# Fixed roles for the banks of PSUM in an attention kernel, with scores in pairs and singles

## The chip, the core and the metric

The kernel runs on one core of a Trainium2 chip. The core has a matrix engine (TensorE, "PE" in the profile, with its weight loads as "PEld"), a vector engine (VectorE, "DVE"), a scalar engine (ScalarE, "ACT"), a general engine (GpSimd, "POOL") and a queue that issues most DMAs (SyncE, "SP"). Matrix products land in PSUM, which has eight banks; one bank holds 512 fp32 values in each of 128 partitions. DVE and ACT read PSUM and write SBUF. The metric is the device time of one execution in microseconds (us); lower is better.

## The reference

The input `x` is 8 sequences of 1024 tokens with 256 features, in fp32. One layer of attention and one feed-forward layer with three-valued weights, each between two layer norms:

```python
x = x + _layernorm(attn(_layernorm(x)))
x = x + _layernorm(ffn(_layernorm(x)))

# attn: 16 heads of 16 features, 4 key/value heads, each shared by 4 query heads
q, k, v = x @ Wq, x @ Wk, x @ Wv          # then rotary embedding of q and k
scores = einsum('bhqd,bhkd->bhqk', q, k) / sqrt(256)
p = softmax(scores, axis=-1)
o = einsum('bhqk,bhkd->bhqd', p, v)        # then o @ Wo

# ffn: weights are +1, 0 or -1 by a threshold
out = einsum('bsd,od->bso', x, ternary(weight) * alpha) + bias
```

## The kernel before

**Units, blocks, steps.** The 8 sequences are cut into 16 units of 512 tokens. A unit has 4 blocks of 4 query heads; a block has 8 steps, one for each 128 keys; a step has 4 score tiles of 128 keys by 512 queries, one for each key/value head. So there are 64 blocks and 2048 score tiles, numbered by `s`.

**Scores are computed twice.** The softmax subtracts each row's maximum. For this a first pass (`max_scores`, line L582, tiles `sm`) makes 128 queries by 512 keys at a time and DVE takes the maximum of each row (`TENSOR_REDUCE`, L607). When a block has all its maxima, they are joined (`mc`, L624), transposed on PE (`shift_rows`, tile `pm`, L630), split in a high and a low part (`mh`, `ml`) and written by a DMA as extra rows into the stacked queries `q_st`. The second pass (`exp_scores`, L655, tiles `se`) then makes 128 keys by 512 queries with the shift already taken off, and ACT takes the exponential (`exp_one`, L671) into an SBUF tile `e`. `av_piece` (L691) multiplies `e` with the values into one PSUM bank `av`; `av_out` (L704) copies it out at the end of a block. There are 2048 matmuls for maxima and 2048 for exponentials. Each uses 64 rows of the array (the other 64 belong to the other pair of key/value heads, index `a`), so two that stand side by side with different `a` run at the same time.

**Groups.** `window(s)` writes out one group: two or three exponentials, as many matmuls for maxima between them, then perhaps one part of other work, then the `av` products of the group two before. PE, DVE and ACT execute exactly in the order in which the Python code calls them. `window_size` takes three exponentials, or two if a part that needs a PSUM bank is ready. Such parts ("banked") come from the projection of a later unit (`x`, `kv_and_dram`, `q`, `v`), from the tail of an earlier one (`attn`, `x`, `ffn`) and from `shift_rows`. The lists `P_PARTS` and `T_PARTS` give the step at which each part becomes ready. `maxima_by` keeps the maxima 40 to 52 score tiles ahead of the exponentials. From `s = 40` on (`REGULAR`) a group takes at most one banked part, and only if it has two exponentials; the last 13 steps have no maxima and take four exponentials at a time (`exp_two`). POOL and SP are ordered by a scheduler, with the hint `issue_after` for DMAs.

**PSUM.** Two tiles of two banks (`sm`) hold scores for maxima, each tile two matmuls; three single banks (`se`) hold scores for exponentials and, in turn with them, the results of banked parts; one bank is `av`. If a group ends between the two matmuls of an `sm` tile, `reduce_early` has DVE reduce the first half by itself, and the second half later.

The code follows with the profile's line numbers.

## Time and profile before

| | |
|---|---|
| median of 3 runs | 1646.88 us (1641.69 to 1648.25) |
| the profiled execution's own time | 1642.63 us |
| its span, first to last instruction | 1640.8 us |
| PE busy | 1579.7 us (96%) |
| DVE busy | 1399.3 us (85%) |
| ACT busy | 1274.8 us (78%) |
| POOL busy | 835.4 us (51%) |

A line of the profile's table of groups names the source line, the engine, the operation, the tile written and the tiles read, the shape, and how often it ran; after the bar stand the busy time of the group, the mean duration of one in ns, and the idle time of the engine just before, with what ended it. PE is pipelined: a matmul's recorded duration is longer than its turn, and the distance from one start to the next is what counts. In a timeline, the first column is the start in us and the second the time from the first start to the last end of the instructions merged into that line.

### The profile page before, as it was taken

What the parts mean: (1) busy time and instruction counts of PE and PEld (TensorE: products, weight loads), DVE (VectorE), ACT (ScalarE), POOL (GpSimd) and SP (SyncE); (2) the same over time, 40 slices, a digit from 0 to 9 for tenths busy, and PEclk for the clock granted to TensorE, in tenths of its full rate; (3) what the DMA queues carried; (4) which work ended last, traced back from release to release, by engine and by line L of the source; (5) the groups of instructions that cost most, each with busy time, mean ns of one, the idle gap of its engine ahead of it and who ended that gap; (6) DMA issues with size and microseconds to landing.
All of it is one profiled execution on the core that took longest, in us unless ns stands there. A gap on an engine that the chain in (4) does not pass through costs nothing.

```text
span 1640.8 us, 37250 instructions
## 1 busy us (share of the span) xinstructions
PE 1579.7 (96%) x14712; PEld 818.5 (50%) x14712; DVE 1399.3 (85%) x2049; ACT 1274.8 (78%) x2479; POOL 835.4 (51%) x1239
## 2 busy tenths in 40 slices
PE   7999999999999999999999999999999999999997
PEld 5544455454545545454544545455454544444544
DVE  7778788889898888989889898988989888898964
ACT  4657778878787887878788787887878787877884
POOL 5532457374653737455373835547374552323363
PEclk8989999999999999999999999999999999999999
DMA  4151425125151422515133251513325151231100
GB/s 139 53 101 34 91 77 101 59 76 101 56 106 49 91 67 82 101 46 105 60 83 75 77 106 44 104 49 89 71 67 104 40 97 42 46 70 34 42 15 27
DMA packets 86079, 117.99 MB, mean 72 GB/s; under 512 B 12088, under 2 KB 50808, under 8 KB 85752
## 3 DMA queue, kind: packets, MB, share of 16 engines
q1 hardware_dynamic: 85904, 115.60, 29.9%
q8 instruction: 116, 1.90, 0.5%
q14 instruction: 59, 0.48, 0.1%
HBM read 68.65 MB, written 45.88 MB: 70 GB/s over the span
## 4 chain that ended last, share of the span: by engine, by line
PE 80%; DVE 10%; DMA 3%; ACT 2%; POOL 2%; issue 2%; SPq 1%; POOLq 0%; DVEq 0%; ACTq 0%
PE av L691 28%; PE se L655 28%; PE sm L582 9%; DVE mx L607 7%; PE pa L283 3%; PE pq L283 2%; PE pf L283 2%; PE pt_ot L267 2%; ACT e L671 2%; PE pt_xt L267 2%; PE pkv L283 2%; DMA q_st<-ml 1%; DMA k_rot<-d_k 1%; PE pm L630 1%; DMA dk<-ks 1%
## 5 line engine op out<-in xcount | busy, mean ns | idle before, releaser
L607 DVE TENSOR_REDUCE mx<-sm 128x2 f32<-128x1024 f32 (+1 forms) x1304 | 1205.3, 973 | 191.9 <-PE sm L582 174.1
L671 ACT ACTIVATE e<-se 128x512 f32<-128x512 f32 x1996 | 1058.2, 602 | 223.0 <-PE sm L582 172.4
L582 PE MATMUL sm<-k_st,q_st 64*128 64x512 f32 x2048 | 748.4, 450 | 6.9 <-DVE mx L607 3.9
L655 PE MATMUL se<-q_st,k_st 64*128 64x512 f32 x2048 | 705.5, 441 | 26.7 <-ACT e L671 14.4
L691 PE MATMUL av<-e,v_aug 128*32 128x256 f32 (+3 forms) x8608 | 607.2, 378 | 0.0
L655 PEld LDWEIGHTS se<-q_st,k_st 64*128 64x128 f32 x2048 | 324.9, 185 | 405.7 <-ACT e L671 302.1
L582 PEld LDWEIGHTS sm<-k_st,q_st 64*128 64x128 f32 x2048 | 326.1, 185 | 65.1 <-DVE mx L607 41.9
L691 PEld LDWEIGHTS av<-e,v_aug 128*32 128x32 f32 x8608 | 194.4, 108 | 211.0 <-issue 148.3
L241 POOL TENSOR_SCALAR lnsc<-mv 128x2 f32<-128x2 f32 (+1 forms) x134 | 25.8, 193 | 400.1 <-DVE mv L239 395.1
L765 POOL TENSOR_TENSOR xn<-xn,a 128x512 f32<-128x512 f32 x30 | 38.4, 1282 | 131.8 <-DMA a<-d_rec 101.2
L826 POOL TENSOR_TENSOR a<-a,bias_bc 128x512 f32<-128x512 f32 x30 | 38.6, 1287 | 108.3 <-ACT a L825 108.3
L242 POOL TENSOR_TENSOR lnsc<-lnsc,mhalf 128x2 f32<-128x2 f32 (+1 forms) x134 | 92.5, 691 | 0.9
L162 POOL TENSOR_TENSOR hl<-xn,hl 128x512 fp32r<-128x512 f32 x60 | 76.5, 1287 | 0.4
L253 POOL TENSOR_SCALAR xn<-x,lnsc 128x256 f32<-128x256 f32 x116 | 65.1, 570 | 2.2
L237 DVE BATCH_NORM_STATS2 bnst<-a 128x6 f32<-128x256 f32 x120 | 44.5, 413 | 4.6 <-POOL a L826 4.6
L297 POOL TENSOR_TENSOR t<-q_rot,sin_q_sb 128x512 f32<-128x512 f32 x31 | 39.9, 1288 | 15.5 <-ACT q_rot L439 15.4
L283 PE MATMUL pa<-woh,hl 128*128 128x256 f32 x240 | 46.2, 294 | 1.1 <-ACT e L671 1.1
L283 PE MATMUL pq<-xt,wqkvh 128*128 128x256 f32 x256 | 45.8, 303 | 0.5 <-ACT e L671 0.5
L237 DVE BATCH_NORM_STATS2 bnst<-x 128x6 f32<-128x256 f32 x124 | 45.9, 412 | 0.4 <-DMA x<-in_L_attn_x 0.4
L271 ACT CAST ot<-pt_ot 128x512 fp32r<-128x512 f32 x66 | 39.6, 601 | 4.7 <-PE pt_ot L267 4.7
L439 ACT COPY q_rot<-pq 128x512 f32<-128x512 f32 x32 | 18.8, 586 | 30.9 <-PE pq L283 30.9
L162 POOL TENSOR_TENSOR hlq<-q_rot,hlq 128x512 fp32r<-128x512 f32 x31 | 39.8, 1285 | 4.8 <-ACT hlq L159 4.5
(157 smaller groups left out, 1303.1 us busy)
## 6 DMA issues: line engine op xcount, KB each, us to landing
q_st<-dq SPq DMA_DIRECT2D x90, 256.0 KB
dq<-hlq SPq DMA_DIRECT2D x60, 256.0 KB
d_av<-avsb SPq DMA_DIRECT2D x60, 256.0 KB
x<-in_L_attn_x SPq DMA_DIRECT2D x15, 512.0 KB
xn<-d_av SPq DMA_DIRECT2D x30, 256.0 KB
a<-d_rec SPq DMA_DIRECT2D x30, 256.0 KB
xr<-in_L_attn_x SPq DMA_DIRECT2D x15, 512.0 KB
out_x<-a SPq DMA_DIRECT2D x30, 256.0 KB
```

The costliest lines, as they stand in the source:

```text
L162: eng.tensor_tensor(lo, src, hi.bitcast(F32), ALU.subtract)
L237: nc.vector.bn_stats(st[:, t, :], src[:, t, :])
L242: nc.gpsimd.tensor_tensor(sc[:, 1, :], sc[:, 1, :], mhalf[:, :n], ALU.pow)
L253: eng.tensor_scalar(dst[:, t, :], src[:, t, :], sc[:, 0, t : t + 1] if eng is nc.gpsimd else mv[:, t, 0:1], sc[:, 1, t : t + 1], ALU.add i ...
L267: nc.tensor.transpose(pt[:, c, t * P : (t + 1) * P], src[:, t, c * P : (c + 1) * P], ident_r)
L283: nc.tensor.matmul(out, chunk(left[i], c), chunk(right[j], c), start=(k == 0), stop=(k == len(steps) - 1),)
L297: eng.tensor_tensor(dst, x, table.unsqueeze(1).to_broadcast(list(x.shape)), ALU.mult)
L582: scores = nc.tensor.matmul(sm[0][:, part, :], queries[rows], k_st[(u // UPB) % 3][rows, r2, ch * 512 : (ch + 1) * 512], start=True, stop= ...
L607: early[0] = nc.vector.tensor_reduce(mx[i][:, a, head_and_tile(i, r2, t), lo:n], sm[0][:, lo:n, :], AX.X, ALU.max).ins
L655: nc.tensor.matmul(sc if len(queries.shape) == 2 else sc.rearrange("p (j t) -> p j t", j=G), k_st[(i // G // UPB) % 3][rows, r2, kt * P : ...
L671: nc.scalar.activation(e, sc, AF.Exp, scale=1.0 / D**0.5)
L691: nc.tensor.matmul(av_ps[0][32 * r : 32 * r + 32, lo:hi], va[:, kt, r, :], es[i * NK + kt, r // 2, r % 2][:, lo:hi], start=(kt == 0 and lo ...
```

## The change

The eight banks get fixed roles: one two-bank tile for a pair of scores for maxima (`PAIR_M`, tag `s2`, one buffer), two single banks for single scores for maxima (`ONE`, tag `s1`), one two-bank tile for a pair of scores for exponentials (`PAIR_E`, tag `e2`, one buffer), one single bank for a third exponential or a part's result (`ALONE`, tag `se`), and `av`. The exponential of a pair is one ACT instruction of 128x1024. A group makes its pair of exponentials first, then the pair for maxima, then the single ones. `maxima_of` says how many maxima a group takes: beside one of the parts in `LONG` a group of two takes four (two pairs), other groups of two take two, and groups of three take what is then missing, one at least. The choice of the maxima's order (`pairs`, `singles`) is kept in lists. Some projection parts become ready a few steps later, and from unit 5 on two of them (`kt`, `q_to_dram`) issue their DMAs behind the latest shift.

```diff
-    ep = ctx.enter_context(tc.tile_pool(name="ep", bufs=12))
-    avp = ctx.enter_context(tc.tile_pool(name="avp", bufs=5))
+    ep = ctx.enter_context(tc.tile_pool(name="ep", bufs=4))
+    ep2 = ctx.enter_context(tc.tile_pool(name="ep2", bufs=6))
+    avp = ctx.enter_context(tc.tile_pool(name="avp", bufs=2))
...
-    ps_mx = ctx.enter_context(tc.tile_pool(name="ps_mx", bufs=2, space=PSUM))
-    ps_e = ctx.enter_context(tc.tile_pool(name="ps_e", bufs=3, space=PSUM))
+    ps_mx = ctx.enter_context(tc.tile_pool(name="ps_mx", bufs=1, space=PSUM))
+    ps_s = ctx.enter_context(tc.tile_pool(name="ps_s", bufs=2, space=PSUM))
+    ps_e = ctx.enter_context(tc.tile_pool(name="ps_e", bufs=1, space=PSUM))
...
-    spare = [1]
+    ALONE, ONE = (ps_e, "se"), (ps_s, "s1")
+    PAIR_E, PAIR_M = (ps_e, "e2"), (ps_mx, "s2")
+    spare = [[ALONE, ONE, PAIR_E, ONE, PAIR_M], 0]
...
+    def max_one(a, sm=None):
+        open_block()
...
+        if sm is None:
+            sm = ps_s.tile([P, 512], F32, tag="s1", name=f"s1_{a}_{i}_{t}_{r2}_{ch}")
+        max_scores(item, a, sm)
+        x = head_and_tile(i, r2, t)
+        nc.vector.tensor_reduce(mx[i][:, a, x, ch : ch + 1], sm, AX.X, ALU.max)
+        block_ends(i)
+        return a
+
+    def max_two(a, place=None):
+        open_block()
+        pool, tag = place or PAIR_M
+        sm = pool.tile([P, 2, 512], F32, tag=tag, name=f"s2_{taken[0]}")
...
+        for k in range(2):
+            max_scores(item, (a + k) % 2, sm[:, k])
+        x = head_and_tile(i, r2, t)
+        nc.vector.tensor_reduce(mx[i][:, :: -1 if a else 1, x, ch], sm, AX.X, ALU.max)
+        block_ends(i)
...
-    def exp_one(s):
...
-        nc.scalar.activation(e, sc, AF.Exp, scale=1.0 / D**0.5)
+    def exps_of(s, n, place=None):
+        pool, tag = place or (ALONE if n == 1 else PAIR_E)
+        shape = [P, 2, 512] if n == 2 else [P, 512]
+        sc = pool.tile(shape, F32, tag=tag, name=f"se_{s}")
+        e = (ep2 if n == 2 else ep).tile(shape, F32, tag=f"e{n}", name=f"e_{s}")
+        for k in range(n):
+            step, (r2, a) = (s + k) // 4, divmod((s + k) % 4, 2)
...
+            exp_scores(step, r2, a, sc[:, k] if n == 2 else sc)
         nc.scalar.activation(e, sc, AF.Exp, scale=1.0 / D**0.5)
...
-        (26, "begin", 0), (33, "x", 0, 0), (34, "x", 0, 1), (37, "begin", 1), (43, "x", 1, 0),
-        (45, "x", 1, 1), (49, "kv_and_dram"), (51, "q", 0), (52, "kt"), (53, "v"), (55, "q", 1),
-        (57, "q_to_dram"),
+        (30, "begin", 0), (35, "x", 0, 0), (36, "x", 0, 1), (37, "begin", 1), (43, "x", 1, 0),
+        (45, "x", 1, 1), (49, "kv_and_dram"), (51, "q", 0), (54, "kt"), (53, "v"), (55, "q", 1),
+        (62, "q_to_dram"),
...
-        (1, "fetch"), (7, "invert"), (8, "scale", 0), (9, "scale", 1), (12, "attn", 0),
+        (2, "fetch"), (7, "invert"), (8, "scale", 0), (9, "scale", 1), (12, "attn", 0),
...
+            behind = [behind_latest] if u > 4 and p[0] in ("kt", "q_to_dram") else []
+            at(start + k, *behind, part, projects, u, *p)
...
+    LONG = ("kv_and_dram", "q", "attn", "ffn")
+    AHEAD = 4
+
+    def maxima_of(s, size):
+        time = min(maxima_by(s + size), 4 * NSTEP)
+        n = time - taken[0]
+        if s < REGULAR:
+            return max(0, n)
+        if size == 2:
+            part_ = next((p for p in ready if banked(*p)), None)
+            far = part_ and not at_hand() and part_[0] is part and part_[1][2] in LONG
+            n = 4 if far and taken[0] + 4 <= time + AHEAD else 2
+        else:
+            n = max(1, n)
+        return min(n, 4 * NSTEP - taken[0])
...
         if late:
-            for r2 in range(2):
-                exp_two(s // 4, r2)
+            spare[0] = [ALONE, ONE, ONE]
+            for k in range(0, size, 2):
+                exps_of(s + k, min(2, size - k), PAIR_M if k else None)
         else:
-            end = min(maxima_by(s + size), 4 * NSTEP)
-            for q in range(max(size, end - maxima[0])):
-                if q < size:
-                    exp_one(s + q)
-                if maxima[0] < end:
-                    max_scores(maxima[0])
-                    maxima[0] += 1
-                if q == 0:
-                    take_low()
-            reduce_early(maxima[0])
+            n = maxima_of(s, size)
+            exps_of(s, 2)
+            take_low()
+            half = s % 2
+            if n >= 2:
+                max_two(half)
+                n -= 2
+            if size == 3:
+                exps_of(s + 2, 1)
+            else:
+                half = 1 - half
+            while n:
+                if n == 2:
+                    max_two(1 - half)
+                    break
+                half = max_one(1 - half)
+                n -= 1
...
+        spare[0] = [ALONE]
         while s < 8:
             s = window(s)
```

## The prediction

> **What bounds the kernel now.** I read the page first, for shares and the chain.

> ```profile
> PE 1579.7 (96%) x14712; PEld 818.5 (50%) x14712; DVE 1399.3 (85%) x2049; ACT 1274.8 (78%) x2479; POOL 835.4 (51%) x1239
> ...
> PE 80%; DVE 10%; DMA 3%; ACT 2%; POOL 2%; issue 2%; SPq 1%; POOLq 0%; DVEq 0%; ACTq 0%
> ```

> PE sets the pace and DVE is close behind; ACT has room. Second, the groups by form, for the price of one instruction:

> ```profile
> L671 ACT ACTIVATE e<-se 128x512 f32<-128x512 f32 x1996 | 1058.2, 602 | 223.0 <-PE sm L582 172.4 <-PE se L655 31.8
> L607 DVE TENSOR_REDUCE mx<-sm 128x2 f32<-128x1024 f32 x712 | 855.3, 1216 | 167.5 <-PE sm L582 153.2 <-PE se L655 11.0
> L607 DVE TENSOR_REDUCE mx<-sm 128x1 f32<-128x512 f32 x592 | 381.9, 680 | 24.5 <-PE sm L582 20.9
> ```

> A reduction of a pair takes 1.216 us, a half 0.680. Third, the waits, for what PE waits for:

> ```profile
> PEld se L655 <- ACT e L671: 302.1, 651, 0.9
> ...
> PEld sm L582 <- DVE mx L607: 41.9, 127, 1.4
> ...
> PE se L655 <- DMA q_st<-ml: 9.9, 8, 3.1
> ```

> The first is mostly no loss: the weight load waits while the av products still run. The second is real: over the whole run PE waits only 41.9 us for a maxima bank. Fourth, the timeline of PE, for the length of a group (first se to first se):

> ```profile
> 1003.28 0.50 PE L655 MATMUL se<-q_st,k_st 64*128 64x512 f32 x1
> 1003.29 0.50 PE L582 MATMUL sm<-k_st,q_st 64*128 64x512 f32 x1
> 1003.62 0.48 PE L655 MATMUL se<-q_st,k_st 64*128 64x512 f32 x1
> 1003.62 0.48 PE L582 MATMUL sm<-k_st,q_st 64*128 64x512 f32 x1
> 1004.10 0.74 PE L283 MATMUL pkv<-xt,wqkvh 128*128 128x256 f32 x4
> ...
> 1006.50 0.50 PE L655 MATMUL se<-q_st,k_st 64*128 64x512 f32 x1
> 1006.51 0.50 PE L582 MATMUL sm<-k_st,q_st 64*128 64x512 f32 x1
> 1006.84 0.39 PE L655 MATMUL se<-q_st,k_st 64*128 64x512 f32 x1
> 1006.84 0.62 PE L582 MATMUL sm<-k_st,q_st 64*128 64x512 f32 x2
> 1007.07 0.39 PE L655 MATMUL se<-q_st,k_st 64*128 64x512 f32 x1
> 1007.40 0.85 PE L691 MATMUL av<-e,v_aug 128*32 128x384 f32 x8
> 1008.18 0.49 PE L655 MATMUL se<-q_st,k_st 64*128 64x512 f32 x1
> ```

> Two scores run side by side (1006.50 and 1006.51); the next two follow after 0.34 us, the third two after 0.23, other work 0.33 after the last. av takes 0.78 here (1007.40 to 1008.18), 0.57 for 256 columns. So a plain group (three exponentials, three maxima) needs 1.68 us of PE, or 1.46 with the shorter av, and the long one at 1003.28 took 3.22. And DVE beside it:

> ```profile
> 1005.37 0.74 DVE L237 BATCH_NORM_STATS2 bnst<-a 128x6 f32<-128x256 f32 x2
> 1006.03 0.30 DVE L239 BATCH_NORM_AGGREGATE mv<-bnst 128x2 f32<-128x6 f32 x2
> 1007.30 1.23 DVE L607 TENSOR_REDUCE mx<-sm 128x2 f32<-128x1024 f32 x1 [0.97 <-PE sm L582]
> ```

> The reduction starts at 1007.30, 0.46 us after its second score's start (1006.84); DVE idled 0.97 beside the long part. Cutting all PE rows so, I count 449 plain groups, mean 1.806; of groups of two, 13 with pkv (mean 3.21), 26 pq (3.22), 31 pa (2.99), 28 pf (2.55), 61 pm (1.655), 109 with a transposition (1.98), 29 without a part (1.56), 13 ptv (1.47). A plain group's maxima cost DVE 1.73 start to start (1.131 a pair, 0.597 a half), about PE's 1.68: plain groups are where DVE binds, long ones where it idles.

> **The change part by part.** The changed order keeps the cuts between groups and their parts. Instead of 449 plain groups it has 367 with three maxima and 81 with one; 81 groups of two take four maxima (28 pa, 14 pf, 13 pkv, 12 pq, 14 pm); some 229 groups of two keep one pair. Matmuls and maxima are the same in number.

> (A) The 81 groups with four. Both pairs are written to the one s2 tile, so the second waits for DVE's reduction of the first, and all of PE's queue stands behind it: the long part, the av products, the next group. First pair at 0.34; reduction 0.46 later, at 0.80; it ends at 2.02; the second pair starts 0.05 later (a matmul started at 1010.03 after a reduction that ended at 1009.98), at 2.07; the part 0.33 later, at 2.40. Before, the part started at 0.66. That is 1.74 us per group, 81 x 1.74 = +141 us. Bounds: 1.41 if the second pair's own 0.33 is given back whole (+114), 2.34 if DVE is a single reduction late (0.60) on arrival (+190).

> (B) The 81 groups of three that then take one maximum use no s2; PE needs 0.34 + 0.33 + 0.57 or 0.78 = 1.24 to 1.45. The pair tile for exponentials has one buffer too: 0.53 from the matmul to ACT (1006.50 to 1007.04), about 1.01 for 128x1024 (an estimate: copies of 256 and 512 columns take 380 and 586 ns, so 0.41 more for 512 more), 0.05 to the next: 1.60. I take 1.51 against 1.806, -24 us; bounds 1.24 (-46) and 1.60 (-17).

> (C) The 367 plain groups. One s2 tile makes a round of 0.46 + 1.216 + 0.054 = 1.73 from pair to pair, and the single reduction just fits beside the pair's fetch; DVE's other work comes on top. That is 141 us in all (244 statistics x 0.33, 256 aggregates x 0.11, the 64 joins, 64 low parts and 15 reciprocals); half in these groups is 0.19 each, some of it beside waits. I take 1.86 against 1.806: +20. Bounds 1.73 (-28) and 1.90 (+34).

> (D) Groups of two with one pair meet the round of 1.73 as well: pm +0.08 x 47, no part +0.17 x 29, ptv +0.26 x 13, the rest is longer already; +12, bounds 0 and +25.

> (E) `av_out` puts its copy (0.47 start to start) ahead of the pair's exponential 63 times: 1.60 + 0.47 = 2.07 against a group of 1.8. Three buffers hid this; with one it costs up to 0.27 each. Half meets a wait for s2 anyway: +10, bounds 0 and +25.

> (F) Before `s = 40` all parts share one bank instead of three, several in one group: +8, bounds 0 and +15.

> (G) Moved steps. `begin 0` (two statistics and two aggregates on DVE, seven instructions on POOL), `kt` (six on POOL, ten DMAs on SP), `q_to_dram` (four DMAs) and the tail's `fetch` (three) come later. q_st is reloaded some 35 steps after `q_to_dram`, and k_st is read some 60 after `kt`, so SP's and POOL's delay is hidden; at one step of about 2.9 us that cover is over 100 us. Keeping these DMAs out of the shift's way can win at most the 9.9 us row: -5, bounds -10 and 0. The fewer SBUF tiles cost nothing: an avsb buffer is reused two blocks later (some 46 us, for one DMA of 256 KB), a pair of `e` six groups later, and its last av product comes four groups later. If av fell two groups further behind, that cover would be gone and ACT would wait a group.

> (H) Merging exponentials saves ACT 0.956 - 0.89 = 0.07 a pair, some 735 times, 48 us of ACT's time. ACT is 78% busy and 2% of the chain: nothing, and a pair's first half is now released 0.4 later, which stands in B and E.

> Sum: 141 - 24 + 20 + 12 + 10 + 8 - 5 = +162 us. The profiled execution took 1642.6 us (span 1640.8 and 1.8 around it), 4.3 under the median of the runs; 1642.6 + 162 = 1805, on the median 1809.

> [...] The rows say that two tiles of maxima left 41.9 us of waits in 2048 scores. [...] For ACT, the rows of H give 0.07 us a merge. [...]

> **The rivals.** (1) A milder loss: after each stall DVE and ACT have caught up, so B and C fall to their lower ends, and A to its own: 114 - 46 - 28 + 12 + 10 + 8 - 5 = +65, 1712. For it: DVE's 0.97 of idle beside the pkv group. Against: the round of 1.73 leaves no group with a pair below it. (2) Faster: the four maxima beside a long part do what DVE's idle time invites. If the second pair waited little, A would be 81 x 0.23 = 19, and with B at -46, C at -28, the rest nil and G at -5, -60: 1587. It decides at a wait where A is below 79 us, 0.97 us a group; the reduction alone is 1.22. (3) ACT's one pair tile binds: exponentials that follow a copy of a part (0.59) also miss the next group, some 160 times 0.3, +48: 1857. (4) The change doesn't do what it says: if the part is rarely beside the four, A vanishes; but the order shows all 81.

> Stalls might also cost clock. Here PEclk stays at 9 after the third slice, through a 3.06 us gap of PE at 198.5 us; the new ones are 1.4. [...]

> **How the numbers follow.** Forecast case 0.70; rival 1 0.14; rival 2 0.05; rival 3 0.08; rival 4 or no change 0.03. The range runs from rival 1 to beyond rival 3, 1705 to 1870, and leaves out rival 2, rival 4 and what exceeds A's upper bound. Faster by over 0.5% (about what a measurement here can tell) 0.06, within it 0.02, slower 0.92.

> **What will show it.** Right: PE waits for DVE before the second pair, some 1.3 us, in 81 groups, over 100 us in all against 41.9; PE's and DVE's busy shares fall together; plain groups stay near 1.8. Wrong: that wait below 50 us, plain groups at 1.68 or less, or a large new wait of se for ACT.

## The result and the profile after

| | before | after |
|---|---|---|
| median | 1646.95 us (4 runs, 1641.69 to 1648.25) | 1885.14 us (4 runs, 1882.93 to 1888.08) |
| ratio, 95% interval | | 1.1454 (1.1425 to 1.1484) |
| span of the profiled execution | 1640.8 us | 1881.1 us |
| granted TensorE clock, mean | 0.989 | 0.954 |

The change is 238 us slower. The forecast was 1809 us, range 1705 to 1870: the sign and most of the mechanism were right, but the size was 76 us short, and the time lies above the range.

The page after: busy shares, the granted clock in 40 slices, and the shares of the chain that ended last. (In the changed kernel L598 is `max_scores`, L638 the reduction of a pair and L621 that of a single score, L676 `exp_scores`, L695 the exponential, L705 `av_piece` and L296 the parts' products.)

```profile
PE 1680.6 (89%) x14456; PEld 810.2 (43%) x14456; DVE 1428.1 (76%) x1987; ACT 1232.4 (66%) x1683; POOL 835.5 (44%) x1239
...
PEclk8899989999898999989989999998999999999989
...
PE 55%; DVE 31%; ACT 7%; issue 2%; POOL 2%; DMA 2%; SPq 0%; ACTq 0%; POOLq 0%; DVEq 0%
```

All engines' shares fall together, and DVE's part of the chain goes from 10% to 31%: PE now waits for reductions. New are the 8s of the clock after the third slice. Before, that row was

```profile
PEclk8989999999999999999999999999999999999999
```

The waits of PE and of its weight loads (total us, times, longest):

```profile
PEld se L676 <- ACT e L695: 320.8, 632, 1.3
...
PEld s L598 <- DVE mx L638: 284.2, 559, 2.0
...
PE s L598 <- DVE mx L638: 131.9, 124, 1.6
```

The last two rows are waits of a score for maxima for DVE. PE's own wait is 131.9 us in 124 places, where before it was 3.9 us. The 284.2 us are waits of the weight loads, 41.9 before; a weight load can wait while PE still multiplies (before the scores for exponentials the weight loads waited 320.8 us for ACT, PE itself 15.5), so the two rows must not be added up to a loss. The groups by form show that the instructions themselves have hardly changed; only the merged exponential is new:

```profile
L638 DVE TENSOR_REDUCE mx<-s 128x2 f32<-128x1024 f32 x790 | 965.0, 1223 | 287.7 <-PE s L598 281.4 <-PE se L676 2.9
L695 ACT ACTIVATE e<-se 128x1024 f32<-128x1024 f32 x796 | 816.2, 1027 | 326.8 <-PE se L676 315.7 <-PE s L598 2.8
```

One group with four maxima, in the timeline of PE (start, us, engine, operation, idle before):

```profile
1029.42 0.50 PE L676 MATMUL se<-q_st,k_st 64*128 64x512 f32 x2
1029.75 0.40 PE L598 MATMUL s<-k_st,q_st 64*128 64x512 f32 x2
1031.47 0.50 PE L598 MATMUL s<-k_st,q_st 64*128 64x512 f32 x2 [1.32 <-DVE mx L638]
1031.90 0.50 PE L296 MATMUL pa<-woh,hl 128*128 128x256 f32 x2
1033.53 0.64 PE L705 MATMUL av<-e,v_aug 128*32 128x256 f32 x8
1034.10 0.50 PE L676 MATMUL se<-q_st,k_st 64*128 64x512 f32 x2
```

The second pair starts 1.72 us after the first, with PE idle for 1.32 of it, and the products of the part `attn` stand behind it: term A as it was drawn. The windows give the clock of this group and of one ten microseconds later (length, then busy time of PE, PEld, DVE, ACT, POOL, then PEclk, DMA share, GB/s):

```profile
1029.40:1034.10 4.70, 3.38 (x31) 2.16 (x28) 2.55 (x3) 1.48 (x3) 0.00 (x0) 1.00 0.01 3
1039.15:1045.60 6.45, 5.12 (x34) 3.31 (x34) 4.25 (x8) 2.05 (x3) 1.32 (x4) 0.75 0.00 0
```

The second one has the same 1.32 us of waiting, but half of it ran at half clock: the part's products that took 1.63 us (1031.90 to 1033.53) take 2.38 there, and the group 6.45 us.

```profile
1041.78 0.50 PE L296 MATMUL pa<-woh,hl 128*128 128x256 f32 x2
...
1044.16 1.51 PE L705 MATMUL av<-e,v_aug 128*32 128x256 f32 x16
```

### The profile page after: what moved, and what is told of

It is laid out like the page before. It is cut to its first block, busy times and chain, and to the rows that moved or that the text cites. A ratio compares the mean times of both kernels' runs of the same rounds, so it can differ in the third digit from the quotient of the medians.

```text
span 1881.1 us, 36120 instructions
## 1 busy us (share of the span) xinstructions
PE 1680.6 (89%) x14456; PEld 810.2 (43%) x14456; DVE 1428.1 (76%) x1987; ACT 1232.4 (66%) x1683; POOL 835.5 (44%) x1239
## 3 DMA queue, kind: packets, MB, share of 16 engines
q8 instruction: 114, 1.87, 0.4%
## 4 chain that ended last, share of the span: by engine, by line
PE 55%; DVE 31%; ACT 7%; issue 2%; POOL 2%; DMA 2%; SPq 0%; ACTq 0%; POOLq 0%; DVEq 0%
DVE mx L638 22%; PE av L705 17%; PE se L676 14%; PE s L598 11%; ACT e L695 7%; DVE mx L621 6%; PE pa L296 3%; PE pq L296 3%; DVE bnst L250 2%; PE pkv L296 2%; PE pt_ot L280 1%; PE pf L296 1%; PE pt_xt L280 1%; DVE mv L252 1%; PE pm L651 1%
## 5 line engine op out<-in xcount | busy, mean ns | idle before, releaser
L695 ACT ACTIVATE e<-se 128x1024 f32<-128x1024 f32 (+1 forms) x1252 | 1041.9, 870 | 336.7 <-PE se L676 318.4
L638 DVE TENSOR_REDUCE mx<-s 128x2 f32<-128x1024 f32 x790 | 965.0, 1223 | 287.7 <-PE s L598 281.4
L598 PE MATMUL s<-k_st,q_st 64*128 64x512 f32 x2048 | 511.0, 461 | 143.9 <-DVE mx L638 131.9
L705 PE MATMUL av<-e,v_aug 128*32 128x256 f32 (+3 forms) x8352 | 633.6, 395 | 1.7 <-ACT e L695 0.9
L676 PE MATMUL se<-q_st,k_st 64*128 64x512 f32 x2048 | 579.9, 483 | 33.1 <-ACT e L695 15.5
L676 PEld LDWEIGHTS se<-q_st,k_st 64*128 64x128 f32 x2048 | 233.3, 187 | 425.3 <-ACT e L695 320.8
L621 DVE TENSOR_REDUCE mx<-s 128x1 f32<-128x512 f32 x468 | 318.9, 682 | 124.0 <-PE s L598 109.1
L598 PEld LDWEIGHTS s<-k_st,q_st 64*128 64x128 f32 x2048 | 219.5, 188 | 294.8 <-DVE mx L638 284.2
L705 PEld LDWEIGHTS av<-e,v_aug 128*32 128x32 f32 x8352 | 192.4, 110 | 231.0 <-issue 163.1
L806 ACT COPY a<-pa 128x512 f32<-128x512 f32 x30 | 17.6, 586 | 87.8 <-PE pa L296 80.7
L296 PE MATMUL pq<-xt,wqkvh 128*128 128x256 f32 x256 | 51.6, 331 | 1.3 <-DVE ml L660 1.3
L296 PE MATMUL pa<-woh,hl 128*128 128x256 f32 x240 | 51.2, 320 | 0.0
L839 ACT ACTIVATE a<-pf,alpha_bc 128x512 f32<-128x512 f32 x30 | 20.7, 690 | 42.4 <-PE pf L296 41.0
```

Of the source, the lines that this page charges most:

```text
L296: nc.tensor.matmul(out, chunk(left[i], c), chunk(right[j], c), start=(k == 0), stop=(k == len(steps) - 1),)
L598: nc.tensor.matmul(sm, queries[rows], keys, start=True, stop=True)
L621: nc.vector.tensor_reduce(mx[i][:, a, x, ch : ch + 1], sm, AX.X, ALU.max)
L638: nc.vector.tensor_reduce(mx[i][:, :: -1 if a else 1, x, ch], sm, AX.X, ALU.max)
L676: nc.tensor.matmul(sc if len(queries.shape) == 2 else sc.rearrange("p (j t) -> p j t", j=G), k_st[(i // G // UPB) % 3][rows, r2, kt * P : ...
L695: nc.scalar.activation(e, sc, AF.Exp, scale=1.0 / D**0.5)
```

## The experiments

In all of them the time of a group is taken as in the prediction, from PE's rows: start of its first `se` to start of the next group's. Nothing of the computation is left out anywhere; one run adds matmuls that nobody reads. Unless another base is named, the ratio is to the kernel before, with its 95% interval. Groups are named by the tile of the part beside them: `pkv`, `pq` and `ptv` belong to the projection (`kv_and_dram`, `q`, `v`), `pa` and `pf` to the tail (`attn`, `ffn`), `pm` to `shift_rows`, and a transposition to the parts `x`. A plain group has three exponentials, three maxima and no part. E and M stand for a score for an exponential and for a maximum, so EE MM EM is the order of the changed kernel's plain group.

### What the groups of four cost, and how

**No group of four**, the rest of the change as it is:

```diff
-    AHEAD = 4
+    AHEAD = -4 * NSTEP
```

> The fixed banks stay, but every group of two takes two maxima, so no group waits for its own first pair. Theory (the second pair's wait of 1.32 us in 81 groups and the half clock that follows it carry the loss): the 81 long groups fall from 425 us in sum to the 223 of before, 448 plain groups at 1.89 cost 36 more than before, other groups of two and the start some 24: 1647 + 36 + 24, about 1705. Rival (the single pair tiles hurt every group, the groups with four are a small part): above 1800.

1697.1 us, 1.0314 (1.0294 to 1.0335). So the groups of four cost 188 us and the fixed roles without them 50.

**Work for PE in the wait.** The wait stays; six matmuls into the `se` bank, with an output that nothing reads, fill it:

```diff
                 if n == 2:
+                    if size == 2:
+                        filler = ps_e.tile([P, QKV], F32, tag="se", name=f"filler_{s}")
+                        for _ in range(6):
+                            nc.tensor.matmul(filler, ident_r, wqkv_s[0][:, 0], start=True, stop=True)
                     max_two(1 - half)
```

> The wait stays, and PE is given six matmuls of 384 columns (into the bank for single exponentials, read by nobody) to run during it, about 1.0 of the 1.32 us. Theory with the clock: after the first 100 us the changed kernel ran 148 us at half clock against 6 before; that goes, and 148/2, about 70 us, with it: 1810 to 1825. Without the clock as a cause: 1885 or a little more, since the matmuls only add work.

1832.21 us, 1.1135 (1.1115 to 1.1156): 53 us faster than the change by giving PE useless work. Its page and one of its groups:

```profile
PE 1730.0 (95%) x14942; PEld 860.1 (47%) x14942; DVE 1428.1 (78%) x1987; ACT 1232.5 (67%) x1683; POOL 835.7 (46%) x1239
...
PEclk8899999999999999999999999999999999999999
```

```profile
1015.88 0.40 PE L598 MATMUL s<-k_st,q_st 64*128 64x512 f32 x2
1016.21 1.32 PE L1178 MATMUL filler<-wqkvh,ident_r 128*128 128x384 f32 x6
1017.61 0.51 PE L598 MATMUL s<-k_st,q_st 64*128 64x512 f32 x2
```

The second pair still starts 1.73 us after the first, and the clock's 8s behind the first slices are gone (mean 0.990). So the 53 us are clock. The wait itself stays: the 81 groups of four take 425.4 us in the change, 377.9 here, and groups of the same kinds took 223.1 before.

**The second pair behind the long part**, and **four maxima as a pair and two singles**, so that no second pair waits for the one tile:

```diff
+            later = None
...
-                    max_two(1 - half)
+                    if size == 2:
+                        later = 1 - half
+                    else:
+                        max_two(1 - half)
...
         do_parts(3 - size if REGULAR <= s < ends else 99)
+        if not late and later is not None:
+            max_two(later)
```

> Groups with four maxima issue the second pair after the long part, not before it, so that DVE reduces the first pair beside the part's 1.6 us; all else as changed. Theory: the wait of 1.32 us and the half clock go, B, C, D and F of the prediction stay: 1647 + 30 + 14 + 10 and up to 24 less for the groups with one maximum, 1680 to 1700. Rival (single pair tiles hurt every group): above 1800.

```diff
-                if n == 2:
+                if n == 2 and size == 3:
```

> Groups with four maxima take the second two as two single scores in the two single banks, still ahead of the long part. Theory: these banks are free, so PE doesn't wait; DVE has 0.06 us more a group: 1680 to 1705, as the run with the pair behind the part. If four maxima beside a part are bad for another reason than the shared tile (DVE late afterwards), it stays above 1800.

1759.85 us, 1.0698 (1.0672 to 1.0722), and 1727.81 us, 1.0498 (1.0479 to 1.0516). Both beat the change and both missed: without groups of four at all it is 1697. In the second, the long groups still grow (beside pa 3.50 us against 2.99 before, beside pq 3.83 against 3.23), while the 81 groups with one maximum take 1.737 and give back little. In the first, the part is no longer behind the wait, but `av` is: 3.54 us beside pa and 4.37 beside pq. Its clock still halves too, in 12 stretches, 44 us in all, between 101 us and the last 45 us of the span, against its expectation that the half clock goes.

**Four maxima in the kernel before**, with its own order and banks, two more beside the same parts:

```diff
-        if i > 0 and v % 2:
+        if i > 0 and v % 2 and not reduced:
...
+            long_ = next((p for p in ready if banked(*p)), None)
+            if s >= REGULAR and size == 2 and long_ and long_[0] is part:
+                if long_[1][2] in ("kv_and_dram", "q", "attn", "ffn"):
+                    end = min(end + 2, 4 * NSTEP)
```

> The kernel before, in its own order and banks, with two more maxima beside kv_and_dram, q, attn and ffn, and two fewer in the groups that follow. Theory (DVE's idle time beside long parts can be used where the tiles are double): 1625 to 1645. Rival (the two more matmuls of a long group don't find a partner with other rows and run one after the other, and the next group's don't either): 1650 to 1670.

1758.08 us, 1.0684 (1.0662 to 1.0705), beyond the rival too. The clock is in it (mean 0.966; 23 stretches, 85 us, at half clock in the middle of the run), and groups beside pf take 5.37 us against 2.55. So it is not only the one tile that makes four maxima dear.

### What the fixed roles cost without groups of four

**The moved steps**, undone in the run without groups of four, and done alone in the kernel before (`P_PARTS`, `T_PARTS`, the step of `begin_project` and `behind_latest`; the same lines both times):

```diff
-        (30, "begin", 0), (35, "x", 0, 0), (36, "x", 0, 1), (37, "begin", 1), (43, "x", 1, 0),
+        (26, "begin", 0), (33, "x", 0, 0), (34, "x", 0, 1), (37, "begin", 1), (43, "x", 1, 0),
...
-            behind = [behind_latest] if u > 4 and p[0] in ("kt", "q_to_dram") else []
+            behind = []
```

> As the run without groups of four, but the projection's parts, the tail's fetch and the DMAs of kt and q_to_dram stand where they stood before. Theory (the moved steps gain at most the 9.9 us that PE waited for the shift's DMA): 1697 to 1707. Rival (the moved steps are a part of the 51 us that were left against the kernel before): below 1690.

> The kernel before with only the moved steps and the DMAs issued behind the latest shift. Theory: between 10 us less and no change, 1636 to 1646. Rival (moved steps cost): above 1650.

1704.79 us (1.0364, 1.0337 to 1.0390): undoing them costs 8. But alone in the kernel before they cost 8: 1652.69 us (1.0048, 1.0031 to 1.0064). Their sign depends on the rest.

**Two pair tiles for maxima** (a single score takes half of one), and **exponentials in three single banks**, one instruction each:

```diff
-    ps_mx = ctx.enter_context(tc.tile_pool(name="ps_mx", bufs=1, space=PSUM))
-    ps_s = ctx.enter_context(tc.tile_pool(name="ps_s", bufs=2, space=PSUM))
+    ps_mx = ctx.enter_context(tc.tile_pool(name="ps_mx", bufs=2, space=PSUM))
...
-    ALONE, ONE = (ps_e, "se"), (ps_s, "s1")
+    ALONE, ONE = (ps_e, "se"), (ps_mx, "s2")
```

> As the run without groups of four, but the tile of pairs for maxima has two buffers, and a single score for maxima takes half of one (the two single banks for maxima are given up; eight banks as before). Theory (the round of 0.46 + 1.22 + 0.05 on one pair tile, and the 0.11 us that PE loses at each restart behind it, hold the plain groups at 1.87): plain groups fall towards 1.80, 448 x 0.07, about 1665. Rival (the single pair tile for exponentials, whose round is 1.61, holds them): 1690 or more.

```diff
-    ps_e = ctx.enter_context(tc.tile_pool(name="ps_e", bufs=1, space=PSUM))
+    ps_e = ctx.enter_context(tc.tile_pool(name="ps_e", bufs=3, space=PSUM))
...
-        nc.scalar.activation(e, sc, AF.Exp, scale=1.0 / D**0.5)
+        for k in range(n):
+            nc.scalar.activation(e[:, k] if n == 2 else e, sc[k], AF.Exp, scale=1.0 / D**0.5)
```

> As the run without groups of four, but exponentials go to three single banks in turn, shared with the parts' results as before, with one ACT instruction each; the banks for maxima are those of the changed kernel. Rival (the pair tile for exponentials and the merged ACT instruction hold the groups): the floor of 1.61 goes, groups of 256 av columns fall to 1.46, below 1670. Theory (the pair tile for maxima holds them): 1685 to 1700.

1697.48 us (1.0317, 1.0291 to 1.0343) and 1712.0 us (1.0410, 1.0378 to 1.0441). Neither gained. The first made groups with a part faster (beside pm 1.686, was 1.837) and plain ones slower (1.944, was 1.869); the second has plain groups of 1.828, but its start (up to the first plain group) is 17 us longer. The parts and the first maxima use other banks there; which of it costs the time was not taken apart.

**Both together, the banks of before under the changed order** (the last two diffs), then with groups of four again (`AHEAD = 4`):

> The changed order (pair of exponentials, pair for maxima, singles; no groups of four) on the old banks: two tiles of pairs for maxima, a single score taking half of one, and three single banks for exponentials and parts, one ACT instruction for each. Theory (the two single pair tiles hold the groups, each masking the other, so that freeing one alone showed nothing): back to 1645 to 1660. Rival (the order itself costs the 51 us that are left): 1685 or more.

> As the run before it in this list, with the groups of four maxima beside long parts. The second pair now finds a free tile. Theory: no wait of 1.32 us, no half clock, and the groups with one maximum can fall below 1.61: within 15 us of the run without groups of four, on either side. Rival (four maxima beside a part make DVE late for what follows, whatever the tiles): 25 us or more above it.

1701.0 us (1.0342, 1.0314 to 1.0371) and 1732.35 us (1.0525, 1.0505 to 1.0546). Still no gain without groups of four (the start is 13 us longer than in the kernel before), and with them it is 31 us slower, as the second text's rival had it. That left two suspects for the first: the order within a group (two exponentials, two maxima), or the bank that a single score leaves empty in its pair tile.

**The empty bank given to the next group's single score**, and then **to the next score of any kind**, as the kernel before does (a pair is then taken as two singles). Against the run with the old banks:

```diff
+            if shared:
+                whole, first = shared.pop()
+                sm = whole[:, 1]
...
+        one = nc.vector.tensor_reduce(mx[i][:, a, x, ch : ch + 1], sm, AX.X, ALU.max).ins
+        if whole is not None and first is None:
+            shared.append((whole, one))
```

> This is the kernel with the banks of before and the order of the change without groups of four, plus one edit: a single score for maxima no longer takes half of a two-bank tile and leaves the other bank empty; the single scores of two successive groups share one two-bank tile, each still reduced by itself. Theory (the empty bank is what still costs): two tiles hold four scores again as before the change, a score is seldom held up, and a plain group falls from 1.917 us to the 1.81 of before; with 448 of them that is 448 x 0.11 = 49 us less than 1701, so 1645 to 1665 us, the start's 13 us still in it. Rival (the order of the scores within a group, two exponentials first and then two maxima, is what costs): the bank that is gained stays unused when it matters, plain groups stay at 1.88 or more, and the time is 1690 us or more. A time between says that both have a part.

```diff
     def max_two(a, place=None):
         open_block()
+        if shared:
+            max_one(a)
+            max_one(1 - a)
+            return
```

> The kernel with the shared two-bank tile, and one edit more: where a single score has left a bank of its tile empty, the next pair is taken as two single scores, so that the first fills that bank at once, as the kernel before does. The run with the shared tile had plain groups at 1.833 us (1.917 without it), but groups of two lost what was won (beside pm 1.645 to 1.813, beside pkv 3.101 to 3.428, without a part 1.508 to 1.685), since the tile with the empty bank was kept from their pair. Theory (the room for scores is what is lost): groups of two come back to their old times, 61 x 0.17 + 13 x 0.33 + 29 x 0.18 + 13 x 0.33 + 57 x 0.08 + 31 x 0.14 = 33 us less than 1698, some 1660 to 1672, the start's 14 us still in it. Rival (the order EE MM EM costs by itself): room is no matter, the loss moves once more, and the time is 1690 us or more.

1698.18 us (1.0315, 1.0287 to 1.0344), then 1670.04 us (1.0134, 1.0102 to 1.0166). The first moved the loss: plain groups 1.917 to 1.833, but groups of two up (beside pm 1.645 to 1.813), because the half-filled tile was kept from their pair. The second won 28 us.

**The same flow of maxima, with the change's merged exponentials and their one pair tile** (the last two diffs on the run with two pair tiles for maxima):

> The scores for maxima flow into two tiles with every bank filled at once, as in the run of 1670 us, but the exponentials keep the change's banks: one pair tile with one instruction for two, and a single bank. The start is the change's own, some 13 us shorter than in the run of 1670 us. Theory (only the room for maxima was lost): 1655 to 1662 us, a plain group at 1.825. Rival (the one pair tile of the exponentials holds the groups by itself, as the floor of 1.61 in groups with one score suggests): nothing is won on the 1697 us of the run without groups of four, 1685 us or more.

1669.8 us (1.0144, 1.0120 to 1.0167), between theory and rival: 27 us better than the run without groups of four, so the maxima's banks are about half of its loss of 50 us. Against the run of 1670.04 us, which has the same flow of maxima and single banks for exponentials, nothing is won or lost: the start is 9.5 us shorter, but no plain group is below 1.614 us (1.459 there) and their mean is 1.862 (1.825 there).

**The order alone, in the kernel before:**

```diff
-            for q in range(max(size, end - maxima[0])):
-                if q < size:
-                    exp_one(s + q)
-                if maxima[0] < end:
...
+            exp_one(s)
+            exp_one(s + 1)
+            take_low()
+            for q in range(2, max(size, end - maxima[0] + 1)):
+                for _ in range(2 if q == 2 else 1):
...
-        n, (a, r2) = s // 4, divmod(s % 4, 2)
+        n, (r2, a) = s // 4, divmod(s % 4, 2)
```

> The kernel before with its banks, its exponentials one by one, its steps and its scores written one after the other into two-bank tiles; only the order within a group is that of the change: two exponentials first, then two scores for maxima, then the third of each. For this the pair of an exponential alternates between the halves of the array, as in the change, and the two scores of a tile are the two halves of one key range. Theory (the room for scores is what was lost, the order is harmless): within 10 us of the kernel before, 1637 to 1657, plain groups at 1.80. Rival (the order costs by itself): the loss that the run with the old banks kept, 54 us less the 13 of its start, so 1680 us or more, with plain groups at 1.88 or more.

1676.08 us (1.0171, 1.0135 to 1.0207), but this order has a cost of its own: the third exponential and the third score lie in the same half of the array and run one after the other (starts 0.56 and 0.80 us into the group). With the two scores of a tile exchanged, and then with the moved steps added:

```diff
-        a, ch, t, r2 = part if i else 1 - part, k // NK, k // 2 % UT, k % 2
+        a, ch, t, r2 = 1 - part, k // NK, k // 2 % UT, k % 2
```

> The run with the order alone had a fault of its own: in its plain groups the third exponential and the third score for maxima lie in the same half of the array, so they do not run side by side (starts at 0.56 and 0.80 in place of 0.57 and 0.58), 0.23 us in each of 449 plain groups, 103 us at most where PE sets the end. Its plain groups took 1.916 us against 1.806, 49 us more, and its groups of two 16 us less than before. Here the two scores of a tile change places, so that the third score lies in the other half. Theory (the order EE MM EM is harmless, the room is what the change lost): plain groups fall back to 1.80 or less and the time to 1625 to 1650 us. Rival (the order costs by itself): plain groups stay at 1.88 or more, 1670 us or more.

> The run before this one with the change's moved steps added. In the kernel before the moved steps cost 8 us, in the changed one without groups of four they gained 8. If it is the order that makes them pay, this is some 8 us below the run with the order alone; if it is the banks, some 8 us above it.

1651.57 us (1.0039, 1.0024 to 1.0055) and 1650.65 us (1.0027, 1.0008 to 1.0047). The order is nearly harmless, 4 to 9 us by the interval, and the moved steps on top of it do nothing that can be told.

**Groups of four with the room they lacked**, in the run in which every bank is filled:

```diff
-    AHEAD = -4 * NSTEP
+    AHEAD = 4
```

> The run in which the next pair fills the empty bank (1670 us), with groups of four taken again beside the long parts. There is room for four scores now, so no second pair waits for the reduction of the first if DVE has kept up, and a group of three with one score has no floor from a merged pair of exponentials. Theory (the groups of four lose by the missing room): a long group grows by the 0.23 us that its second pair needs, 81 x 0.23 = 19 us, the 81 groups with one score fall from 1.825 to about 1.45, 81 x 0.37 = 30 us, and the time is 1655 to 1665 us. Rival (DVE comes late out of the plain groups, and the second pair then waits ahead of the part, room or not): as with the old banks and half-filled tiles, where the groups of four cost 31 us more than they gave, 1690 us or more.

1715.05 us (1.0410, 1.0390 to 1.0431): 45 us slower than without them. The rival's time was right. One of its long groups, beside pa, in a window of the same columns as above, and the wait of its second pair:

```profile
1044.36:1048.22 3.86, 3.58 (x38) 2.40 (x34) 3.86 (x7) 2.09 (x4) 0.00 (x0) 1.00 0.00 0
```

```profile
1044.69 0.40 PE L599 MATMUL s<-k_st,q_st 64*128 64x512 f32 x2
1045.37 0.50 PE L599 MATMUL s<-k_st,q_st 64*128 64x512 f32 x2 [0.28 <-DVE mx L630]
```

DVE is busy for all 3.86 us. And in the kernel before, the windows of groups beside pkv, pq, and two beside pa:

```profile
1003.28:1006.50 3.22, 3.22 (x36) 2.28 (x32) 3.05 (x6) 2.33 (x5) 0.53 (x2) 1.00 0.24 87
1009.81:1013.10 3.29, 3.29 (x36) 2.38 (x32) 3.29 (x7) 2.15 (x4) 0.56 (x2) 1.00 0.52 158
...
989.04:991.89 2.85, 2.85 (x28) 1.94 (x25) 1.26 (x2) 1.61 (x4) 0.81 (x1) 1.00 0.04 12
996.90:999.98 3.08, 3.08 (x38) 2.21 (x34) 3.05 (x6) 1.94 (x4) 0.00 (x0) 1.00 0.00 0
```

DVE (third of the busy times) idles 0.17, 0.00, 1.59 and 0.03 us there. Over all groups that later take four it idles 0.82 us beside pa, 0.32 beside pq, 0.21 beside pkv, 0.08 beside pf, 0.03 beside pm (DVE's rows joined within each group): weighted by 28, 12, 13, 14 and 14 that is 31 us in 81 groups, 0.38 each. A pair more costs DVE 1.13 (start to start, in the kernel before). The difference is 81 x 0.75 = 61 us, and in the last run the long groups did grow by 61 us (284.8 us, against 223.4 for 81 groups of the same kinds without four). The groups with one maximum gave back 25 (1.513 us against 1.825), and plain groups lost 16 (1.868 against 1.825).

That the two sums agree so well is partly luck, since kind by kind they don't: this account has a group grow by 0.31 us beside pa, 0.81 beside pq, 0.92 beside pkv, 1.05 beside pf and 1.10 beside pm, and measured are 0.57, 0.52, 0.43, 1.64 and 0.77. Some 19 us of the 61 are the second pair's own turn on PE (81 x 0.23). PE's waits for DVE before a score for maxima grow from 20.6 to 42.2 us over the run, 13 of them in the 14 groups beside pf. So that DVE has little room beside the long parts is measured; that this is the whole of what the groups of four cost where tiles are free is argued, and no run gave DVE less to do there.

## Why the prediction was wrong, and where it was right

**The step that failed is the clock.** The prediction asked whether stalls might cost clock, let a stall of 1.4 us pass because a gap of 3.06 us had left PEclk at 9, and put no term for it into the sum or into the range. The runs show 28 stretches at half clock, and with the 1.32 us waits filled these stretches and 53 us are gone. The filled run takes 1832 us, 23 above the forecast and inside the range; as run, the changed kernel lies 15 us above it.

**A second premise failed without moving the sum:** "plain groups are where DVE binds, long ones where it idles" was read from one wait of 0.97 us behind one long group. The windows and means above show DVE nearly full in most long groups. So the prediction knew one reason for the loss, the one tile, where there is more, and the experiments that only removed the tile's wait missed by 20 to 60 us. One reading was wrong too: the 41.9 us that "PE waits" for a maxima bank are waits of its weight loads, and PE's own were 3.9 us.

Point by point, group means of the changed kernel against those of before, times their number:

| term | predicted | measured |
|---|---|---|
| A, 81 groups of four | +141 | +155 with the wait filled (377.9 - 223.1), +202 as run |
| clock | none | 48 of these 202; 53 in all |
| B, 81 groups with one maximum | -24 | -2 (1.778 against 1.806) |
| C, 367 plain groups | +20 | +30 (1.887) |
| D, pm, no part, ptv | +12 | +13 (1.769, 1.719, 1.689) |
| other groups of two | (E +10) | -7 |
| start, up to the first plain group | (in F +8) | +2 (72.9 against 71.1) |
| G, moved steps | -5 | -8 by undoing them (inside the rows above) |
| rest (span +240 in all) | | +3 |

A's mechanism and place were right, its size 9% low. After the clock, B is the term that is furthest off, by 22 us. It took 1.51 for a group, while the exponentials' one pair tile holds it: 0.53 from matmul to ACT, 1.027 us of ACT and 0.05 to the next give 1.61, and the shortest such group in the trace takes 1.613. B called that sum, 1.60, its upper bound, but it is a floor, and the mean of 1.778 lies above it; 0.04 of this goes with the filled wait (1.736), the rest was not taken apart. With three single banks for exponentials and every maxima bank filled the same groups take 1.513, as B had it. C lay within its bounds. D was right. E doesn't show in sum: of the groups that hold the copy of `av`, the 48 plain ones went from 2.10 to 1.98 us, and the 14 with a transposition from 1.92 to 2.20, a rise like E's 0.27. Of F's 8 us the start shows 2. G is right in sign in the changed kernel only.

**The ladder from before to after**, each rung a run, in differences of medians: order 1651.6 (+5); moved steps 1650.7 (-1); merged exponentials in one pair tile with maxima taken in pairs and singles 1669.8 (+19, 5 of them in the start; the same flow of maxima with single banks for exponentials is as slow, 1670.0, with 14 us in the start, so the 19 are not the merging's alone); fixed banks for maxima 1697.1 (+27); groups of four 1885.1 (+188, of which 53 clock). What stays open: why the kernel before gets 6.8% slower when it takes four maxima itself; its clock tells part of it, and no run there filled PE's waits.

**What was to show it**: the wait of 1.32 us in the groups of four, busy shares falling together, over 100 us of waits, all came. "Plain groups stay near 1.8" did not quite (1.887). Rival 3, ACT's pair tile, was partly true: the tile shows as a floor under the short groups.

## What to carry to other kernels

Before work is moved to where an engine "idles", sum that engine's idle time in just those places, window by window: here it was 0.38 us a place for a reduction of 1.13. Count the room that banks with fixed roles can no longer lend: here it was about half of what the roles cost without groups of four, and a half-filled tile was room lost until something filled it (28 us). Price a recurring stall of PE with the clock that it can take from the matmuls behind it, too: here that was 53 us of the 188 that the groups of four cost, and a run that filled the idle stretch with matmuls that nobody reads told it.

## What the runs showed of the hardware

One instruction of 128x1024 on ACT takes 1027 ns, one of 128x512 596: merging saved ACT 42 us of busy time (1274.8 to 1232.4), and none of it is seen in the kernel's time: with the same flow of maxima, the run with merged exponentials and their one pair tile takes 1669.8 us and the one with single banks 1670.0.
